# A planner's lag and the first rotation: moving work between VectorE, ScalarE and GpSimd at the start of an attention and mixture-of-experts kernel

## The chip, the cores and the metric

The kernel runs on one core of one Trainium2 chip. The metric is the device time of one execution in microseconds, given as the median of several executions. The profile shows one execution, with times from the start of its span.

## The reference

Four sequences of 1024 tokens with 256 channels go through a layer norm, attention with 16 heads of 16 channels and rotary positions, an output projection, a layer norm and a residual sum. Then follows a layer norm, a mixture of 8 experts of which each token takes the two most distant centroids, a layer norm and a residual sum.

```python
def apply_rope(x):
    ...
    x1, x2 = (x[..., :half], x[..., half:])
    return jnp.concatenate([x1 * cos - x2 * sin, x1 * sin + x2 * cos], axis=-1)
q = (x @ Wq.T + bq).reshape(B, T, H, D)
k = (x @ Wk.T + bk).reshape(B, T, H, D)
v = (x @ Wv.T + bv).reshape(B, T, H, D)
q = apply_rope(q)
k = apply_rope(k)
scores = jnp.einsum('bthd,bshd->bhts', q, k) / np.sqrt(D).astype(x.dtype)
attn = jax.nn.softmax(scores, axis=-1)
out = jnp.einsum('bhts,bshd->bthd', attn, v).reshape(B, T, C)
return out @ Wo.T + bo
```

The expert part is `silu(xs @ Wg[e] + bg[e]) * (xs @ W1[e] + b1[e]) @ W2[e] + b2[e]`, weighted by a softmax of the two chosen distances.

## The kernel before

Attention comes first, for four batches `b`, each with four groups `g` of four heads. A group needs six things in a row. `project` multiplies the normalized, transposed tokens by the query and key weights, and ScalarE copies the result into `turned`. `rotated` adds the bias and applies the rotary positions in five elementwise instructions (`rot`, two `sw`, `rot`, `rot`) for one half of the sequence (512 tokens, `half` 0 or 1) of one group. `split_up` then makes four copies of each of queries and keys: the value cast to a shorter mantissa, the remainder, and both again in an order in which a matmul of the stacked parts gives the full product. That is four instructions for the queries and four for the keys, and the tile is `split`. `stack` transposes the split on TensorE (`ps`), and copies it to `stack`. `maxima` multiplies queries by keys for the row maxima (TensorE `pm`, VectorE `part`, one `peaks()` for two of each), and `rows` turns them into a `shift`. After that, `scores` recomputes the product with the shift (`sc`), ScalarE takes the exponentials (`e`) and TensorE the weighted sums (`av`) with the value tiles `v_aug`. These are 128x512 tiles cleared once by GpSimd, with a column of ones, into which ScalarE copies the values (`pv`).

The beginning is written out by hand. `prepare(..., fast=True)` for both halves of batch 0 runs layer norm statistics on VectorE (`st_a`, then `mv_a`, `var_a`, and the inverse root up to `off_a`), normalization on ScalarE (`xn`), transposes (`pt`), and the projection of group 0 only. `compact` packs weights on ScalarE, `small_constants` makes constants on VectorE, and `turned_constants` prepares `bias_qk` and `turn`. Then `split` and `stack` of group 0 are finished for both halves. Before the change `split` runs half 0 of this first group on GpSimd and half 1 on VectorE, all other groups on GpSimd.

From there on the order of TensorE, VectorE and ScalarE is that of the program text (a manual schedule), and GpSimd's instructions that go through `pool` keep their order too. Other GpSimd instructions, the clearing of the value tiles among them, are placed by the framework's scheduler, which takes the earliest in the program among those that it believes ready. What is in the program text is decided by a planner in Python that keeps one clock for each engine, `free`. Everything beside scores, maxima and weighted sums is a `Work`: a generator that yields, ahead of each part, the costs of the part by engine in ns, as `"G5500"` for 5500 ns of GpSimd or `"P430 A550"` for TensorE followed by ScalarE. `run_one` takes the first of the works, sorted by due time, whose next part fits: its `ready` time must not lie beyond the engine's clock, and the engine may not be booked further ahead of TensorE's clock than `ROOM`. After a part, `ready` is the part's end plus a `LAG` of its engine:

```python
    ROOM = dict(P=10**9, D=1400, A=2600, G=15000)
    LAG = dict(P=280, D=120, A=150, G=200, W=0)
...
            if self.ready > (now if first in "PW" else max(now, free[first])):
                return False
            return all(e == "W" or free[e] + c - now <= ROOM[e] for e, c in costs)
```

So before the change the second part of a work does not fit directly behind its first part on the same engine: `ready` is one lag beyond the clock, until something else moves the clock. A later instruction in another engine's queue waits on the chip for whatever it needs; the planner does not model when a dependent work on another engine has really ended, only that it has been issued.

After attention come the last two blocks' `finish` and `settle` (output projection, layer norms, choice of experts, and the indirect writes of tokens to `rows`), then the expert part over 46 tiles, and the last layer norm.

Of the kernel before, what the change touches and what calls it, by code (L numbers as in the profile page):

```python
# [8 lines left out]
F32 = mybir.dt.float32  # L9
# [7 lines left out]
P = 128  # L17
B, T, C = 4, 1024, 256
NH, HD = 16, 16
NG = 4  # L20
NT = T // P
# [35 lines left out]
def sandwich(  # L57
# [4 lines left out]
    nc = tc.nc  # L62
# [9 lines left out]
    ap1 = attn.enter_context(tc.tile_pool(name="ap1", bufs=1))  # L72
# [54 lines left out]
    def counting(n, name, step=1, per_partition=0):  # L127

        i = ap1.tile([P, n], I32, tag="sq", name=f"i_{name}")
        nc.gpsimd.iota(i, pattern=[[step, n]], base=0, channel_multiplier=per_partition)  # L130
        f = const.tile([P, n], F32, tag=name, name=name)
        nc.gpsimd.tensor_copy(f, i)
        return f
# [6 lines left out]
    zero = ap1.tile([P, 4 * P], F32, tag="oT", name="zero")  # L140
    nc.gpsimd.memset(zero, 0.0)

    v_aug = []
    for t in range(NT):
        v = ap1.tile([P, NH, 32], F32, tag=f"v{t}", name=f"v{t}")
        nc.gpsimd.memset(v, 0.0)
        nc.gpsimd.memset(v[:, :, HD : HD + 1], 1.0)
        v_aug.append(v)  # L150
    tiles_at = counting(P, "tiles_at")
    region = counting(NE, "region", step=CAP)
    part_id = counting(1, "part_id", per_partition=1)
# [151 lines left out]
    seen = const.tile([P, NE], F32, tag="seen", name="seen")  # L305
    nc.gpsimd.memset(seen, 0.0)

    class InOrder:


# [6 lines left out]
    pool = InOrder(nc.gpsimd)  # L317
# [67 lines left out]
    def bank_free(r, n):  # L385
        return max(ring[r][(taken[r] + i) % len(ring[r])] for i in range(n))

    def take(r, until):
        ring[r][taken[r] % len(ring[r])] = until
        taken[r] += 1  # L390

    ROOM = dict(P=10**9, D=1400, A=2600, G=15000)
    LAG = dict(P=280, D=120, A=150, G=200, W=0)
# [3 lines left out]
    class Work:  # L397
# [21 lines left out]
        def run(self):  # L419
            t = self.ready  # L420
            bank_used = self.need[0] == "P"
            if bank_used:
                r = self.costs()[1][0]
                t = max(t, bank_free(r, 1))
            for e, c in self.costs():
                if e != "W":
                    t = max(t, free[e], free["P"] - 300)
                    free[e] = t + c
                t += c + LAG[e]
            if bank_used:  # L430
                take(r, t)
            self.ready = t
            self.need = next(self.gen, None)
            if self.need is None:
                works.remove(self)

        def finish(self):
            for w in self.after:
                w.finish()
            while self.need is not None:  # L440
                self.run()
# [89 lines left out]
    def rotated(b, g, half, e):  # L531

        c = ap2.tile([P, NTB, 8, HD], F32, tag="rot", name=f"rot_{b}_{g}_{half}")
        sw = ap1.tile([P, NTB, 8, 2, HD // 2], F32, tag="B", name=f"sw_{b}_{g}_{half}", bufs=2)
        cols = slice(2 * 4 * HD * g, 2 * 4 * HD * (g + 1))
        at = slice(NTB * half, NTB * half + NTB)
        e.tensor_tensor(
            c.rearrange("p t h d -> p t (h d)"), turned[half][:, :, cols],
            bias_qk[:, None, cols].to_broadcast([P, NTB, 8 * HD]), ALU.add,
        )  # L540
        sh = [P, NTB, 8, HD // 2]
        for s in range(2):
            o = HD // 2 * (1 - s)
            e.tensor_tensor(
                sw[:, :, :, s, :], c[:, :, :, o : o + HD // 2],
                turn[:, at, None, HD + 8 * s : HD + 8 * s + 8].to_broadcast(sh), ALU.mult,
            )
        e.tensor_tensor(
            c, c, turn[:, at, None, :HD].to_broadcast([P, NTB, 8, HD]), ALU.mult
        )  # L550
        flat = c.rearrange("p t h d -> p (t h d)")
        e.tensor_tensor(flat, flat, sw.rearrange("p t h s d -> p (t h s d)"), ALU.add)
        return c

    def split_up(b, g, half, c, e):
        sp_ = ap2.tile([P, NTB, 2, 4, 4, HD], F32R, tag="split", name=f"split_{b}_{g}_{half}")
        for i in range(2):
            full = c[:, :, 4 * i : 4 * i + 4]
            at = lambda n: sp_[:, :, i, :, n, :]
            e.tensor_copy(at(0), full)  # L560
            e.tensor_tensor(at(1), full, at(0), ALU.subtract)
            e.tensor_copy(at(2), at(i))
            e.tensor_copy(at(3), at(1 - i))
        return sp_

    splits = {}

    def split(b, g, half, fast=False):

        e = nc.vector if fast and half else pool  # L570
        yield "G5500"
        c = rotated(b, g, half, e)
        yield "G4000"
        splits[b, g, half] = split_up(b, g, half, c, e)

    def stack(b, g, half, fast=False):

# [595 lines left out]
    def fetch(j):  # L1173
        n = tiles[j]
        e = nc.sync.value_load(tabi[:, 0, j : j + 1], min_val=0, max_val=NE - 1)
        r = nc.sync.value_load(tabi[:, 1, j : j + 1], min_val=0, max_val=NROW - n * P)
        xt = mp.tile([P, NTS, XW], F32, tag="xt", name=f"xt_{j}")
        nc.sync.dma_start(
            out=xt[:, :n], in_=rows[bass.ds(r, n * P), :].rearrange("(i p) c -> p i c", p=P)
        )  # L1180
        w = wpool.tile([P, WW], F32, tag="w", name=f"w_{j}")
        for p, cols in (
            (slice(0, P), slice(0, OR)), (slice(0, FR + 1), slice(OR, WW)),
            (slice(R2, R2 + FR + 1), slice(OR, WW)),
        )[: n + 1]:
            nc.sync.dma_start(
                out=w[p, cols], in_=wall[bass.ds(e, 1), p, cols].rearrange("e p w -> (e p) w")
            )
        return xt, w
# [45 lines left out]
    def down(j, xt, w):  # L1235

        pos = [bank(f"pe_{j}_{i}") for i in range(tiles[j])]
        for i, po in enumerate(pos):
            r = slice(i * R2, i * R2 + FR + 1)
            nc.tensor.matmul(po[:, :C], hr[j % 2][r, :], w[r, OR:], start=True, stop=False)  # L1240
        for i, po in enumerate(pos):
            for f in range(NC):
                nc.tensor.matmul(  # L1243
                    po[:, :C], hs[j % 2][:, f, i * P : (i + 1) * P],
                    w[:, O2 + f * C : O2 + (f + 1) * C], start=False, stop=(f == NC - 1),
                )
            y = mp.tile([P, C], F32, tag=f"y{i}", name=f"yo_{j}_{i}")
            ids = mp.tile([P, 1], I32, tag=f"ids{i}", name=f"ids_{j}_{i}")
            own = sp.tile([P, 1], F32, tag=f"own{i}", name=f"own_{j}_{i}")
            at = xt[:, i, C + 1 : C + 2]  # L1250
            nc.vector.tensor_scalar(
                own, at, float(2 * B * T), float(j * TS), ALU.is_ge, ALU.mult
            )
            nc.vector.tensor_tensor(ids, own, at, ALU.add)
            nc.vector.tensor_scalar(y, po[:, :C], xt[:, i, C : C + 1], None, ALU.mult)  # L1255
            sent = nc.gpsimd.indirect_dma_start(  # L1256
                out=res[:, :],
                out_offset=bass.IndirectOffsetOnAxis(ap=ids, axis=0),
                in_=y,
                in_offset=None,  # L1260
            )
            tc.declare_no_dep(sent.ins, group="results", reason="rows of their own")
            tc.add_to_no_dep_group("results", sent.ins)
            yield
# [12 lines left out]
    with tc.manual_schedule(engines={ET.SP, ET.PE, ET.DVE, ET.Activation}):  # L1277
        ready, last = [fetch(0), fetch(1)], iter(())
        xT = transposed(0, ready[0][0])
        for j in range(MT):  # L1280
# [13 lines left out]
            xT, last = nxt, down(j, xt, w)  # L1294
# [126 lines left out]
```

## Time and profile before

| what | us |
|---|---|
| median of 3 runs | 1761.02 (1759.54 to 1766.38) |
| the profiled execution's own time | 1750.23 |
| its span | 1748.1 |
| first `pm` matmul (row maxima begin) | 42.31 |
| first `sc` matmul (scores begin) | 83.92 |
| last `av` matmuls begin | 1062.61 |
| first expert matmul `pu` on the chain | 1135.30 |

The span is what the engines' instructions cover; the execution's time is 2.1 us longer. In the timelines a line gives the start, the busy time, the engine, the source line, the operation, the output and input by their names, and in brackets the idle time before it and what ended it. `L315` is the line of the helper through which all `pool` instructions pass, so these are told apart by their tiles.

### The profile page before, as it was taken

To read this page: it belongs to the slowest core of one execution; us is meant where nothing else is said; L and a number is where in the kernel's file an instruction comes from. 1 tells how busy PE (TensorE), PEld (TensorE's weight loads), DVE (VectorE), ACT (ScalarE), POOL (GpSimd) and SP (SyncE) were. 2 spreads that over 40 slices of the span, in tenths; PEclk is the share of its full clock that TensorE was granted. 3 is DMA by queue.
4 is the path that set the end of the run, shared out by engine and by line. 5 is a ranking of instruction groups with operands and counts; after the bars stand their busy time and mean duration, and the time that the engine had idled before them with its cause. 6 is when DMAs were issued, how large, how long until landed. Compare 5 with 4: busy or idle time off the path is not lost.

```text
span 1748.1 us, 27778 instructions
## 1 busy us (share of the span) xinstructions
PE 1571.6 (90%) x9702; PEld 1032.8 (59%) x9702; DVE 1062.8 (61%) x2549; ACT 884.2 (51%) x1811; POOL 548.5 (31%) x1058
## 2 busy tenths in 40 slices
PE   3799999999999999999999996199999999999970
PEld 3454455545555545455554443088888888888860
DVE  6487687787787786777787864333333333333338
ACT  2267777778786767676776675021111111122213
POOL 5652434365463454462541223201111111111110
PEclk8899999999999999999999998599999999999995
DMA  8999800001000100000000101544455555578755
GB/s 247 296 301 254 216 28 16 25 25 37 13 14 13 37 21 29 25 1 13 25 29 10 37 13 49 200 172 178 177 186 187 183 186 185 195 280 290 288 191 216
DMA packets 92030, 213.76 MB, mean 122 GB/s; under 512 B 11469, under 2 KB 71092, under 8 KB 86004
## 3 DMA queue, kind: packets, MB, share of 16 engines
q1 hardware_dynamic: 80820, 178.29, 31.1%
q0 software_dynamic: 8768, 25.33, 4.3%
q10 hardware_dynamic: 2304, 8.39, 1.2%
q8 instruction: 76, 1.25, 0.3%
q14 instruction: 62, 0.51, 0.1%
HBM read 148.75 MB, written 80.58 MB: 131 GB/s over the span
## 4 chain that ended last, share of the span: by engine, by line
PE 51%; issue 26%; DVE 12%; POOL 6%; ACT 3%; DMA 2%; SPq 0%; ACTq 0%; POOLq 0%; DVEq 0%
PE av L802 12%; PE pm L644 9%; PE sc L726 7%; DVE part L648 6%; PE sc L733 5%; POOL res L1256 4%; PE pp L510 3%; PE pu L1213 3%; PE ps L585 3%; PE py L833 2%; PE pv L523 1%; PE pd L675 1%; PE pdist L895 1%; PE pe L1243 1%; ACT e L737 1%
## 5 line engine op out<-in xcount | busy, mean ns | idle before, releaser
L648 DVE TENSOR_REDUCE part<-pm 128x1 f32<-128x512 f32 x1024 | 641.4, 682 | 158.4 <-PE pm L644 157.0
L737 ACT ACTIVATE e<-sc 128x512 f32<-128x512 f32 x1024 | 530.5, 603 | 134.4 <-PE sc L733 133.2
L1213 PE MATMUL pu<-xT,w 128*128 128x256 f32 (+3 forms) x2024 | 361.8, 333 | 6.9 <-DMA xt<-rows 4.0
L1213 PEld LDWEIGHTS pu<-xT,w 128*128 128x128 f32 (+1 forms) x2024 | 316.0, 190 | 40.9 <-issue 9.2
L1219 ACT ACTIVATE sil<-pu,w 128x256 f32<-128x256 f32 (+3 forms) x276 | 117.2, 425 | 435.6 <-PE pu L1213 414.1
L644 PE MATMUL pm<-stack,stack 64*128 64x512 f32 x960 | 273.4, 465 | 11.7 <-DVE part L648 8.9
L802 PE MATMUL av<-e,v 128*32 128x512 f32 x2048 | 276.3, 611 | 0.0
L1224 DVE SCALAR_TENSOR_TENSOR h<-pu,w,sil 128x256 f32<-128x256 f32 (+1 forms) x230 | 97.2, 423 | 230.5 <-ACT sil L1219 230.5
L733 PE MATMUL sc<-shift,bring 64*128 64x512 f32 x1024 | 229.0, 402 | 4.1 <-ACT shift L633 4.1
L1256 POOL DMA_INDIRECT res<-yo,ids x71 | 68.1, 959 | 508.6 <-DVE yo L1255 508.6
L726 PE MATMUL sc<-stack,stack 64*128 64x512 f32 x960 | 220.1, 411 | 1.8 <-ACT stack L592 1.0
L644 PEld LDWEIGHTS pm<-stack,stack 64*128 64x128 f32 x960 | 132.6, 185 | 128.3 <-DVE part L648 82.2
L1243 PE MATMUL pe<-w,h 128*128 128x256 f32 x710 | 169.6, 386 | 0.0
L1243 PEld LDWEIGHTS pe<-w,h 128*128 128x128 f32 x710 | 131.0, 190 | 31.2 <-issue 15.2
L726 PEld LDWEIGHTS sc<-stack,stack 64*128 64x128 f32 x960 | 116.2, 187 | 31.8 <-ACT stack L592 8.8
L733 PEld LDWEIGHTS sc<-shift,bring 64*128 64x128 f32 x1024 | 110.2, 187 | 22.8 <-ACT shift L633 7.9
L1255 DVE TENSOR_SCALAR yo<-pe,xt 128x256 f32<-128x256 f32 x71 | 34.3, 483 | 108.4 <-PE pe L1243 108.4
L585 PEld LDWEIGHTS ps<-ident_r,split 128*128 128x128 f32 x512 | 53.1, 145 | 73.4 <-ACT e L737 31.0
L592 ACT CAST stack<-ps 128x512 fp32r<-128x512 f32 x124 | 72.5, 593 | 45.7 <-PE ps L585 43.7
L991 POOL DMA_INDIRECT rows<-xr,to x64 | 63.3, 989 | 71.7 <-DVE to L986 55.7
L585 PE MATMUL ps<-ident_r,split 128*128 128x128 f32 x512 | 69.9, 268 | 16.8 <-POOL split L315 16.8
L802 PEld LDWEIGHTS av<-e,v 128*32 128x32 f32 x2048 | 40.9, 108 | 72.3 <-issue 69.7
(278 smaller groups left out, 1470.5 us busy)
## 6 DMA issues: line engine op xcount, KB each, us to landing
w<-wall SPq DMA_DIRECT2D x46, 2034.0 KB
rows<-empty SPq DMA_DIRECT2D x35, 1032.0 KB
xt<-rows SPq DMA_DIRECT2D x25, 258.0 KB
wall<-in_wg_dram SPq DMA_DIRECT2D x16, 342.0 KB
wall<-in_w_dram SPq DMA_DIRECT2D x16, 320.0 KB
wall<-in_w_dram SPq DMA_DIRECT2D x8, 640.0 KB
xb<-in_x_dram POOLq DMA_DIRECT2D x8, 512.0 KB, 4.3
resid<-xb SPq DMA_DIRECT2D x8, 512.0 KB
```

Source lines behind the costliest of these rows:

```text
L585: nc.tensor.transpose(ps[:, t * P : (t + 1) * P], splits[b, g, half][:, t, is_k, 2 * pr : 2 * pr + 2].rearrange("p h n d -> p (h n d)"), i ...
L644: nc.tensor.matmul(pm, q[r, t * P : (t + 1) * P], k_[r, half * TB : (half + 1) * TB], start=True, stop=True,)
L648: nc.vector.tensor_reduce(part[:, i, 2 * pr + s, half : half + 1], pm, AX.X, ALU.max)
L726: nc.tensor.matmul(sc, k_[r, kb * P : (kb + 1) * P], q[r, qb * TB : (qb + 1) * TB], start=True, stop=False,)
L733: nc.tensor.matmul(scs[s], bring[pr][r, :], shift[u][r, :], start=False, stop=True)
L737: nc.scalar.activation(e, scs[s], AF.Exp, scale=1.0 / HD**0.5)
L802: nc.tensor.matmul(av[32 * j : 32 * j + 32, :], v_aug[kb][:, 4 * g + j, :], es[j], start=(kb == 0), stop=(kb == NT - 1),)
L1213: nc.tensor.matmul(pu[:m, i, :n], w[:, c0 : c0 + m], xT[:, k, :n], start=(k == 0), stop=(k == KC - 1),)
L1219: nc.scalar.activation(sil[:m, :n], pu[:m, 0, :n], AF.Silu, bias=w[:m, OB + f : OB + f + 1])
L1224: nc.vector.scalar_tensor_tensor(h[:, f, :n], pu[:, 1, :n], bias, sil[:, :n], ALU.add, ALU.mult)
L1243: nc.tensor.matmul(po[:, :C], hs[j % 2][:, f, i * P : (i + 1) * P], w[:, O2 + f * C : O2 + (f + 1) * C], start=False, stop=(f == NC - 1),)
L1256: sent = nc.gpsimd.indirect_dma_start(out=res[:, :], out_offset=bass.IndirectOffsetOnAxis(ap=ids, axis=0), in_=y, in_offset=None,)
```

## The change

It does three things. The rotation of the first group goes to VectorE for both halves, and the six casts and copies of each `split_up` there go to ScalarE, with the two subtractions on VectorE; the costs that the planner is told change with it. The clearing of the eight value tiles stands later in the program, behind the other constants that GpSimd makes. And in the planner, a work whose next part begins on the engine on which its last part ended is ready without the lag.

```diff
@@ -140,14 +140,6 @@
     zero = ap1.tile([P, 4 * P], F32, tag="oT", name="zero")
     nc.gpsimd.memset(zero, 0.0)
-    v_aug = []
-    for t in range(NT):
-        v = ap1.tile([P, NH, 32], F32, tag=f"v{t}", name=f"v{t}")
-        nc.gpsimd.memset(v, 0.0)
-        nc.gpsimd.memset(v[:, :, HD : HD + 1], 1.0)
-        v_aug.append(v)
     tiles_at = counting(P, "tiles_at")
@@ -305,6 +297,14 @@
     seen = const.tile([P, NE], F32, tag="seen", name="seen")
     nc.gpsimd.memset(seen, 0.0)
+    v_aug = []
+    for t in range(NT):
+        v = ap1.tile([P, NH, 32], F32, tag=f"v{t}", name=f"v{t}")
+        nc.gpsimd.memset(v, 0.0)
+        nc.gpsimd.memset(v[:, :, HD : HD + 1], 1.0)
+        v_aug.append(v)
     class InOrder:
@@ -427,12 +427,15 @@
                     t = max(t, free[e], free["P"] - 300)
                     free[e] = t + c
                 t += c + LAG[e]
+                last = e
             if bank_used:
                 take(r, t)
-            self.ready = t
             self.need = next(self.gen, None)
             if self.need is None:
                 works.remove(self)
+            elif self.need[0] == last:
+                t -= LAG[last]
+            self.ready = t
@@ -552,26 +555,26 @@
-    def split_up(b, g, half, c, e):
+    def split_up(b, g, half, c, e, copy):
         sp_ = ap2.tile([P, NTB, 2, 4, 4, HD], F32R, tag="split", name=f"split_{b}_{g}_{half}")
         for i in range(2):
             full = c[:, :, 4 * i : 4 * i + 4]
             at = lambda n: sp_[:, :, i, :, n, :]
-            e.tensor_copy(at(0), full)
+            copy(at(0), full)
             e.tensor_tensor(at(1), full, at(0), ALU.subtract)
-            e.tensor_copy(at(2), at(i))
-            e.tensor_copy(at(3), at(1 - i))
+            copy(at(2), at(i))
+            copy(at(3), at(1 - i))
         return sp_
     def split(b, g, half, fast=False):
-        e = nc.vector if fast and half else pool
-        yield "G5500"
+        e, copy = (nc.vector, nc.scalar.copy) if fast else (pool, pool.tensor_copy)
+        yield "D3000" if fast else "G5500"
         c = rotated(b, g, half, e)
-        yield "G4000"
-        splits[b, g, half] = split_up(b, g, half, c, e)
+        yield "D1000 A2200" if fast else "G4000"
+        splits[b, g, half] = split_up(b, g, half, c, e, copy)
```

## The prediction

> **What bounds the kernel now.** I read the windows first, then what TensorE waits for up to the first scores, then the timelines of TensorE, GpSimd and VectorE there. The page's first rows say what an edit away from TensorE can be worth at most:
>
> ```profile
> PE 1571.6 (90%) x9702; PEld 1032.8 (59%) x9702; DVE 1062.8 (61%) x2549; ACT 884.2 (51%) x1811; POOL 548.5 (31%) x1058
> PE   3799999999999999999999996199999999999970
> ```
>
> TensorE is busy in nine tenths or more of nearly every slice. By the windows it is idle for only 26 us of the 976 between 84 and 1060. Time can be had where the first slices are empty. TensorE's waits before the first scores:
>
> ```profile
> PE ps L585 <- POOL split L315: 16.8, 3, 9.1
> PE pt L474 <- ACT xn L356: 16.3, 3, 13.9
> PE pmx L629 <- DVE mx L625: 2.5, 1, 2.5
> ```
>
> The first line is the change's field: TensorE waited 16.8 us in three waits for the split that GpSimd makes. They are 9.1 us at 36.4, 1.5 us at 38.6, and one of 6.2 us later:
>
> ```profile
> 63.15 0.50 PE L644 MATMUL pm<-stack,stack 64*128 64x512 f32 x2
> 69.87 0.75 PE L585 MATMUL ps<-ident_r,split 128*128 128x128 f32 x4 [6.22 <-POOL split L315]
> ```
>
> It belongs to group 1, which stays on GpSimd, where the two halves stand like this:
>
> ```profile
> 57.18 1.26 POOL L315 TENSOR_TENSOR rot<-turned,bias_qk 128x512 f32<-128x512 f32 x1 [18.64 <-ACT turned L515]
> ...
> 62.57 1.27 POOL L315 TENSOR_TENSOR rot<-turned,bias_qk 128x512 f32<-128x512 f32 x1
> ...
> 67.94 0.40 POOL L315 CAST split<-rot 128x256 fp32r<-128x256 f32 x1
> ...
> 71.72 0.40 POOL L315 CAST split<-rot 128x256 fp32r<-128x256 f32 x1
> ```
>
> A new rotation begins at 57.18 and at 62.57, and only then the two splits, at 67.94 and 71.72. Half 0 is rotated at 62.6 and lies there for 5.4 us while half 1 is rotated. The last fence is VectorE, at the head and in the first rotation:
>
> ```profile
> 8.73 1.85 DVE L347 TENSOR_SCALAR var_a<-mv_a 128x4 f32<-128x4 f32 x1
> ...
> 27.33 0.69 DVE L537 TENSOR_TENSOR rot<-turned,bias_qk 128x512 f32<-128x512 f32 x1 [0.79 <-ACT bias_qk L194]
> 28.12 2.15 DVE L544 TENSOR_TENSOR sw<-rot,turn 128x256 f32<-128x256 f32 x2
> 30.31 1.09 DVE L548 TENSOR_TENSOR rot<-rot,turn 128x512 f32<-128x512 f32 x1
> 31.44 1.63 DVE L552 TENSOR_TENSOR rot<-rot,sw 128x512 f32<-128x512 f32 x1
> ```
>
> `var_a` takes 1.85 us where the same form takes 0.17 us at 13.47; GpSimd runs the clearing of the value tiles back to back from 6.17 to 10.63 beside it. The rotation's three full-width instructions take 0.69, 1.09 and 1.63 us for the same number of elements, while GpSimd rotates the other half.
>
> **The planner's lag (part three), where most of the gain is.** With the lag gone, `G4000` of half 0 fits right behind its `G5500`, before half 1's projection is out. GpSimd then runs rotation 0 (57.18 to 62.6), split 0 (3.8 us, to 66.4), rotation 1 (5.4 us, to 71.8), split 1 (to 75.6): the same work in another order. The transposes are ordered by due time behind the same four value projections as now, so TensorE comes to the first of them at 63.65, as before. That transpose needs the queries' half of split 0, done 1.9 us after its start, so at 64.5 and not 69.8: the wait goes from 6.2 to about 0.9 us. What is late next is half 1. Its first transpose (the fifth in all) ran at about 77.9; it now finds its split half done only at 66.4 + 5.4 + 1.9 = 73.7. TensorE would be there at 71 to 72.5 (64.5 plus the 8.0 us that the stretch from 69.87 to 77.9 took, less up to 1.5 us, because two `pv` of 2.04 and 1.63 us there ran after the idle time and later ones take 1.10). So a wait of 1.2 to 2.7 us is left, and the gain is 77.9 - 73.7 = 4.2 us. The sixth transpose needs 75.5 and is reached at 73.7 + 0.4 + 1.0 + 0.45, so in time. From the first scores on TensorE is the bound, and an earlier start carries through. Bounds: nothing, if the planner's room keeps the old order, and 5.4 us, if the fifth transpose is placed later. I take **-4.2**.
>
> **The first rotation (part one).** After: five VectorE instructions without GpSimd beside them, 3 x 0.69 + 2 x 0.43 (a 128x256 `gt` of two inputs takes 0.43) + four gaps of 0.04 = 3.1 us, from 27.33 to 30.4. Then a chain between the two engines for each of queries and keys: ScalarE's cast (0.40 each, from the four `wqk` copies of 128x256 at a mean of 401 ns; 0.31 more for one directly behind), VectorE's subtraction (0.43[...]), the remaining copies. That puts the second subtraction at 32.2 to 32.6. VectorE's queue holds half 1's rotation behind that wait: 32.7 to 35.7. Its casts and subtractions end at 38.0 on VectorE and 38.7 on ScalarE. Now the splits end at 38.5 (GpSimd) and 37.9 (VectorE). So the serial rotation on one engine eats nearly all of what the lost contention gives back. What is gained is order: half 0 is ready at about 33.4, its four transposes (0.43 each) run in the idle time, and only half 1's four are left. They wait for PSUM banks: `stack` copies stand behind the casts in both queues, VectorE's from 38.0 (0.69 each), ScalarE's from 38.7 (0.59), so the first bank in turn comes free at 39.35, and four transposes bring the first `pm` to 41.1, against 42.31. **-1.2**, between +0.5 (copies with strides slower than `wqk`'s) and -2.0.
>
> **The value tiles (part two).** The eight clearings are 8 x 0.51 = 4.1 us of GpSimd. They are moved past the counters' iotas and casts, `empty` (1.82 us, waiting for ScalarE's `wqk` copy until 11.2), the two `natural` DMAs of the GpSimd queue (0.60 and 0.53), `token_id` and `seen`. On SP, the `rows` transfers that need `empty` start at 16.88 behind sixteen `wo` issues that occupy the queue to 16.04, so an earlier `empty` gives nothing there. The tiles are read at 60, so being late costs nothing by itself.
>
> The row says that `var_a` lost 1.68 us to them, at the start of a chain that is tight: the second half's `off_a` at 16.3 holds ScalarE's `xn`, behind which stand all later copies. By the row alone this is -1.7. [...] Today 2.5 us of them, 6.2 to 8.7, lie beside `st_a` statistics, which run at their usual 0.4 us. That cover is gone once they move. Behind 8.7 come `var_a`, `i_a`, `y_a`, `off_a` twice, then 3.4 us of `small_constants`, and blocking a stream of 4.1 us costs up to 4.1 - 1.7 = 2.4 us more than now, 4 at worst if it meets the second `var_a` whole. If it meets only `small_constants`, the copy of `nT` behind it has about 3 us of slack and little is lost. Even `empty` can do it: a `var_a` that is 1.7 us earlier puts the first `off_a` at 11.3, where `empty` now runs from 11.27 to 13.09. So both ends stay: -1.7 and +4. I take **+0.5**, because most placements give back what the row promises.
>
> **The rest of attention.** The lag also changes VectorE's parts: two parts of `settle` or `finish` can now stand in one piece, up to the 1.4 us that `ROOM` allows. That can complete works earlier, and it can put the row maxima behind a burst. Today's waits of `pm` for `part` between 84 and 1090 are 10.0 us in 19, and of `pmx` for `mx` 5.8 us in 4. No row shows the new order; I bound it by -5 and +10 and take 0. At the tail, the final norm's chain on VectorE and ScalarE from 1065 to 1103 is serial and does not change.
>
> **Sum:** -4.2 - 1.2 + 0.5 = -4.9 us. The profiled execution's 1750.2 would become 1745.3. That execution lies 10.8 us under the median of the runs shown, and I carry the difference over to the median: 1761.0 - 4.9 = 1756.1.
>
> **The rivals.** *More is gained:* the value tiles free the head (-1.7), the fifth transpose does not wait (-5.4), rotation -1.5, and some of the 16 us of VectorE waits go (-3): -11.6, about 1749. For it: the waits are there. Against it: every term at its good end. 0.25.
>
> *Little is left:* the clearing meets the second norm chain (+3 to +4) or the split order changes less than I read. About 1760. For it: the `var_a` row shows a full stop. 0.21.
>
> *Slower:* bursts of VectorE parts ahead of the maxima. Each added wait at the mean of today's 19 costs 10.0/19 = 0.53 us of TensorE. Ten of them cancel the gain; it takes 26 to be 0.5% above the median, more than double today's. 30 added give +11, about 1772. For it: VectorE is 72 to 82% busy through attention. Against it: `ROOM` stays at 1.4 us, and the maxima are drawn twelve steps ahead. 0.12.
>
> *Forecast* as worked out, -2.5 to -8.7: 0.42.
>
> **Numbers.** Half a per cent, 8.8 us, is about what a measurement of this kernel can tell from no change; the three runs alone span 6.8 us. Faster by more is the first rival, 0.25; within, the forecast and the second, 0.63; slower, the third, 0.12. The range from 1746 to 1768 takes in the forecast, the second rival and most of the first.
>
> **What would show it.** After: GpSimd's rows of group 1 alternate rotation, split, rotation, split, the wait of `ps` for `split` near 63 is under 2 us, one of 1 to 3 us follows some 8 us later, first `sc` at about 78.5 to 79.5 (83.92 now). First `pm` near 41.6 with the head's 0.5 us in it; GpSimd idle from 27 to 38. `var_a` at 0.17 us, and another VectorE copy or tensor_scalar of over 1 us beside the clearings. Waits of `pm` for `part` near 10 us in the rest of attention. The prediction is wrong if the first scores are not at least 3 us earlier, or if they are and the gain is lost by 1062.

## The result: scores that begin as early as forecast, and a loss in the attention loop

| | before | after |
|---|---|---|
| median of 6 runs each, one chip | 1765.06 us | 1811.47 us (1809.43 to 1818.12) |
| ratio | | 1.0272, 95% interval 1.0248 to 1.0297 |
| span of the profiled execution | 1748.1 us | 1807.4 us |
| first `pm` / first `sc` | 42.31 / 83.92 | 39.40 / 78.56 |
| copy of the first unit's `ou` / of the last of 32 | 119.55 / 1065.21 | 116.79 / 1124.88 |

The forecast was 1756.1, 4.9 us better than before. The kernel came out 2.7% slower, by 46.4 us of the medians. A unit is eight steps of scores for one group and half a sequence, and ends with ScalarE's copy `ou`. By that clock the changed kernel is 2.8 us ahead after the first unit and 59.7 us behind after the last, so the loop lost 62.4 us. That is one execution against one: the profiled execution of before, at 1750.2 us, is a quick one for its kernel, and the difference of the two profiles (59.2 us in time) lies 13 us above that of the medians.

Half of the gain at the start is gone by the end of the first unit: the first `sc` is 5.4 us early, the first `ou` 2.8 us. In between the granted clock of TensorE, as a share of full speed, averages 0.90 (0.95 before), which is 4.0 us of missing clock in place of 1.7.

On the page, the row of busy time and the row of TensorE's slices answer to the two shown first:

```profile
PE 1594.7 (88%) x9702; PEld 1040.0 (58%) x9702; DVE 1072.1 (59%) x2550; ACT 889.1 (49%) x1823; POOL 536.4 (30%) x1045
PE   4899999998989989989998999259999999999970
```

The same 9702 matmuls are busy 23 us longer, and the loop's slices now have eights among the nines. What TensorE waited for up to the first scores, and group 1's transposes there (from TensorE's timeline):

```profile
PE ps L588 <- ACT split L566: 8.4, 3, 4.4
PE ps L588 <- POOL split L315: 4.2, 2, 3.2
...
62.25 0.54 PE L588 MATMUL ps<-ident_r,split 128*128 128x128 f32 x4 [1.00 <-POOL split L315]
...
71.57 0.53 PE L588 MATMUL ps<-ident_r,split 128*128 128x128 f32 x4 [3.15 <-POOL split L315]
```

GpSimd's timeline shows why: the second half's rotation now stands behind the first half's split.

```profile
54.79 1.26 POOL L315 TENSOR_TENSOR rot<-turned,bias_qk 128x512 f32<-128x512 f32 x1 [34.67 <-ACT turned L518]
60.29 0.40 POOL L315 CAST split<-rot 128x256 fp32r<-128x256 f32 x1
...
64.12 1.27 POOL L315 TENSOR_TENSOR rot<-turned,bias_qk 128x512 f32<-128x512 f32 x1
69.64 0.40 POOL L315 CAST split<-rot 128x256 fp32r<-128x256 f32 x1
```

This is the order that the prediction describes: one wait of 6.2 us has become one of 1.0 and one of 3.2, where it had 0.9 and at most 2.7. VectorE at the head:

```profile
8.68 0.17 DVE L347 TENSOR_SCALAR var_a<-mv_a 128x4 f32<-128x4 f32 x1
...
11.25 1.52 DVE L351 TENSOR_SCALAR off_a<-off_a 128x4 f32<-128x4 f32 x1
...
15.71 4.31 DVE L169 TENSOR_SCALAR diag<-ident,bqk 128x64 f32<-128x64 f32 x8
...
26.30 0.69 DVE L540 TENSOR_TENSOR rot<-turned,bias_qk 128x512 f32<-128x512 f32 x1 [0.79 <-ACT bias_qk L186]
...
27.90 0.69 DVE L551 TENSOR_TENSOR rot<-rot,turn 128x512 f32<-128x512 f32 x1
28.62 0.69 DVE L555 TENSOR_TENSOR rot<-rot,sw 128x512 f32<-128x512 f32 x1
```

`var_a` takes 0.17 us in place of 1.85, and the long times have come back at two other groups of tensor_scalars: `off_a` takes 1.52 us (0.17 before) beside `empty` (GpSimd, 10.93 to 12.75), and eight `diag` take 4.31 us (1.40 before) beside the moved clearings (14.3 to 20.1). So `var_a` lost 1.68 us less, and these two lost 1.35 and 2.91 us more. That the clearings would hold up what stands there next was the author's estimate in the prediction; at the head of before one row shows it, `var_a`, which ended at 10.58, beside clearings that ended at 10.63. What the clearings and `empty` did to the path is small: the rotation begins at 26.30 instead of 27.33. Its three full-width instructions take 0.69 us each with GpSimd idle beside them, as forecast (0.69, 1.09 and 1.63 before).

The loss is in the loop. The waits of TensorE and VectorE from 84 us to the end of attention, before (first two lines) and after:

```profile
PE pm L644 <- DVE part L648: 10.0, 19, 1.6
DVE st_m L362 <- POOL xb L315: 2.9, 2, 1.4
```

```profile
PE pm L647 <- DVE part L651: 36.1, 36, 3.3
PE ps L588 <- POOL split L315: 9.9, 2, 5.1
PE sc L729 <- ACT stack L595: 6.8, 3, 4.7
DVE st_m L362 <- POOL xb L315: 16.0, 7, 4.1
DVE st_m L362 <- issue: 4.4, 1, 4.4
```

The columns are the total, the number of waits and the longest. `pm` waits for `part` not many times more often (36 against 19) but for much longer. And a line that was next to nothing is now 16.0 us: VectorE stands still for `xb`. A block is half a sequence (512 tokens), and there are eight. One such place, in the second block, in the joint timeline of after:

```profile
409.08 1.26 POOL L315 TENSOR_TENSOR xb<-xb,outs 128x512 f32<-128x512 f32 x1 [5.26 <-ACT outs L356]
410.37 0.75 DVE L362 BATCH_NORM_STATS2 st_m<-xb 128x6 f32<-128x256 f32 x2 [2.70 <-POOL xb L315]
411.04 2.47 DVE L651 TENSOR_REDUCE part<-pm 128x1 f32<-128x512 f32 x4
...
411.77 0.79 PE L647 MATMUL pm<-stack,stack 64*128 64x512 f32 x1 [2.82 <-DVE part L651]
```

Read from the top: ScalarE is late with the normalized `outs`, for which GpSimd is idle 5.26 us, so its sum `xb` is late; `settle`'s second pair of statistics stands at the head of VectorE's queue and waits 2.70 us for it; the row maxima `part` stand behind it with their inputs ready (the last `pm` ahead of them began at 408.56, `part` at 411.04), and the next `pm` waits 2.82 us for `part`. Before, the last sum of the same block had ended 40 us ahead of its statistics (GpSimd's timeline, then VectorE's):

```profile
369.22 1.27 POOL L315 TENSOR_TENSOR xb<-xb,outs 128x512 f32<-128x512 f32 x1 [0.71 <-ACT outs L356]
...
410.76 0.74 DVE L362 BATCH_NORM_STATS2 st_m<-xb 128x6 f32<-128x256 f32 x2
413.26 0.74 DVE L362 BATCH_NORM_STATS2 st_m<-xb 128x6 f32<-128x256 f32 x2
```

A second price comes with the stall, in the windows around it. The columns are the stretch, its length, each engine's busy time with instructions, and the granted clock of TensorE third from the right:

```profile
408.00:410.80 2.80, 0.95 (x7) 0.50 (x5) 0.43 (x2) 2.80 (x7) 1.26 (x1) 1.00 0.00 0
410.80:417.60 6.80, 5.83 (x16) 2.20 (x17) 3.51 (x12) 1.23 (x3) 2.21 (x12) 0.50 0.24 80
417.60:420.00 2.40, 2.40 (x17) 1.53 (x16) 0.86 (x2) 1.41 (x3) 0.58 (x3) 0.99 0.00 0
```

From 410.8 to 417.6 TensorE has half of its clock (0.50). That is 3.4 us of missing clock, of which 0.5 falls in the wait itself, so by this estimate the wait of 2.82 us costs about as much again. The wait runs from 408.95 to 411.77, and the half clock begins 1.9 us into it.

The windows from the first `ou` to the last, before and then after, account for the loop (the first figure behind the length is TensorE's busy time):

```profile
119.55:1065.21 945.66, 921.52 (x6186) 495.99 (x6186) 723.92 (x1551) 693.25 (x1387) 385.71 (x830) 0.99 0.16 45
```

```profile
116.79:1124.88 1008.09, 943.37 (x6182) 503.15 (x6182) 733.87 (x1555) 693.64 (x1386) 380.83 (x822) 0.96 0.15 42
```

Of the 62.4 us, TensorE is idle for 40.6 (64.7 against 24.1), and busy for 21.9 more with practically the same matmuls. The clock explains the second part: by the trace's clock the busy time misses 31.3 us against 10.2, so 21 more. Of the idle time from 84 to 1060, single waits of 1.7 us or longer make up 39.7 us in 13, against 5.4 us in 3 before; the shorter ones hardly differ (21.6 against 17.3).

The 13 have more than one cause. Nine are waits of `pm` for `part`, 23.3 us in all, of which five stand behind statistics that wait for `xb`. Two are waits of `ps` for a split (9.9 us) and two of `sc` for ScalarE's copy of a stack (6.5 us).

### The profile page after: what moved, and what is told of

It reads as the page before. It is cut to its first block, busy times and chain, and to the rows that moved or that the text cites. A ratio compares the mean times of both kernels' runs of the same rounds, so it can differ in the third digit from the quotient of the medians.

```text
span 1807.4 us, 27782 instructions
## 1 busy us (share of the span) xinstructions
PE 1594.7 (88%) x9702; PEld 1040.0 (58%) x9702; DVE 1072.1 (59%) x2550; ACT 889.1 (49%) x1823; POOL 536.4 (30%) x1045
## 4 chain that ended last, share of the span: by engine, by line
PE 48%; issue 26%; DVE 14%; POOL 6%; ACT 4%; DMA 1%; another core or an unknown queue 0%; SPq 0%; ACTq 0%; POOLq 0%; DVEq 0%
PE av L805 12%; PE pm L647 9%; PE sc L729 6%; DVE part L651 6%; PE sc L736 5%; POOL res L1259 3%; PE pp L513 3%; PE pu L1216 2%; PE ps L588 2%; PE py L836 2%; PE pv L526 1%; ACT e L740 1%; PE pdist L898 1%; PE pd L678 1%; PE pe L1246 1%
## 5 line engine op out<-in xcount | busy, mean ns | idle before, releaser
L647 PE MATMUL pm<-stack,stack 64*128 64x512 f32 x960 | 282.7, 476 | 39.2 <-DVE part L651 34.8
L805 PE MATMUL av<-e,v 128*32 128x512 f32 x2048 | 284.2, 627 | 0.0
```

What stands on the lines that cost most here:

```text
L647: nc.tensor.matmul(pm, q[r, t * P : (t + 1) * P], k_[r, half * TB : (half + 1) * TB], start=True, stop=True,)
L805: nc.tensor.matmul(av[32 * j : 32 * j + 32, :], v_aug[kb][:, 4 * g + j, :], es[j], start=(kb == 0), stop=(kb == NT - 1),)
```

## The experiments

Fourteen kernels ran, in four sets with the kernel before on the same chip. "Loop" below is the change of the last `ou` against the profile of before, less that of the first; one execution against another it is good to about 7 us, since a kernel with the same order on TensorE (the run of the beginning alone) differs by 7.0. The ratios are firmer. The column on `xb` leaves out waits that the trace puts down to "issue".

| run | ratio (95%) | loop us | `st_m` for `xb` us (times) | TensorE waits from 1.7 us up (times) |
|---|---|---|---|---|
| before | 1 | 0 | 2.9 (2) | 5.4 (3) |
| changed kernel | 1.0272 (1.0248 to 1.0297) | +62.4 | 16.0 (7) | 39.7 (13) |
| e1 planner only | 1.0329 (1.0303 to 1.0356) | +64.8 | 16.4 (7) | 38.0 (13) |
| e2 beginning only | 0.9993 (0.9985 to 1.0001) | +7.0 | 2.9 (2) | 9.9 (5) |
| e3 lag off, VectorE | 1.0313 (1.0287 to 1.0339) | +64.9 | 16.0 (7) | 42.8 (10) |
| e4 lag off, GpSimd | 1.0150 (1.0129 to 1.0171) | +35.5 | 2.9 (2) | 24.3 (6) |
| e5 lag off, start | 0.9976 (0.9966 to 0.9986) | -5.6 | 2.9 (2) | 7.5 (4) |
| e6 settle held back | 1.0144 (1.0127 to 1.0161) | +27.5 | none | 23.0 (6) |
| e7 all held back | 1.0033 (1.0017 to 1.0050) | +16.6 | none | 13.2 (3) |
| e14 all but settle held back | 1.0110 (1.0084 to 1.0135) | +29.1 | 12.9 (6) | 16.8 (7) |
| e10 settle joined | 1.0216 (1.0194 to 1.0237) | +31.5 | 8.0 (5) | 30.4 (7) |
| e13 joined, settle held back | 1.0022 (1.0015 to 1.0030) | -4.5 | none | 11.9 (3) |
| e8 ROOM 1300 | 1.0126 (1.0104 to 1.0149) | +23.8 | 5.0 (3) | 17.7 (7) |
| e11 ROOM 1390 | 1.0026 (1.0017 to 1.0036) | +2.5 | 2.9 (2) | 10.7 (3) |
| e12 LAG 1 | 1.0106 (1.0084 to 1.0127) | +22.1 | 8.8 (5) | 16.0 (6) |
| e9 start, and all held back | 0.9953 (0.9938 to 0.9968) | +1.2 | none | 9.3 (2) |

### Which part of the change: e1 to e4

The planner's part alone, on the kernel before; then the other two parts without it (the changed kernel with the old three lines of the planner).

> The kernel before with part three alone (no lag between two parts of a work on one engine). Its TensorE queue is in the order of the changed kernel, entry by entry. All theories: if the loss is part three's alone, 46 us over before plus what the hand-written beginning gives, so +47 to +52 us. If the loss needs the first two parts, within 5 us of before.

> The changed kernel with the old lag: parts one and two alone. TensorE's queue is in the order of before, entry by entry. The changed kernel's first row maxima begin 2.9 us earlier than before (39.4 against 42.3), so -2 to -4 us if an earlier start carries through to the end; 0 if a later wait takes it back.

The planner alone takes 1816.83 us against 1757.55, so it carries the whole loss; TensorE's order in it is that of the changed kernel entry by entry. It loses more than the whole change (59.3 us; 47 to 52 were expected), and why the other two parts are worth that much beside it is not shown. The beginning alone takes 1756.70. Its first `pm` comes at 40.48, 1.8 us early, but without the planner's new order for group 1 the transpose waits 6.25 us for its split as before, and the first `sc` is back at 83.44. So the two parts on their own give next to nothing.

Then the lag was taken away for one engine at a time.

```diff
-            elif self.need[0] == last:
+            elif self.need[0] == last == "D":
```

> The changed kernel with the lag removed only where both parts are on VectorE. Theory A (the lag on GpSimd kept VectorE and TensorE from standing in their queues for GpSimd's results): no loss, -5 to +5 us against before, waits of st_m for GpSimd's xb near 3 us. Theory B (bursts of VectorE parts ahead of the row maxima, the prediction's third rival): most of the loss, +25 to +45. Theory C (any order other than the tuned one is worse): +15 to +45 here and in the GpSimd half alike.

> The changed kernel with the lag removed only where both parts are on GpSimd. Theory A: most of the loss, +30 to +50 us, with waits of st_m for xb and of ps for split as in the changed kernel. Theory B: -8 to +5, the gain of the beginning with little loss. Theory C: +15 to +45, as in the VectorE half.

VectorE's half alone costs as much as everything (1813.61), GpSimd's half about half of it (1784.59). The two do not add up, since each makes a plan of its own, and none of the three theories foretold both. VectorE's half has the stalls for `xb` in full, GpSimd's has none beyond those of before and instead waits of `ps` for the split of up to 8.1 us. That is two kinds of damage: statistics issued ahead of their data, and late splits. The bursts as such, which the prediction's third rival had in mind, exist too: one of the changed kernel's 13 long waits, at 451, stands behind 4.6 us of `settle`'s selection in one piece, planned at 2.0 us (`D400`, twice `D600`, `D400`). One of its instructions, a tensor_scalar whose median over 16 is 0.18 us, takes 1.21 us, with 1.28 us of GpSimd's rotation beside it (447.82 to 449.10):

```profile
447.93 1.21 DVE L938 TENSOR_SCALAR sel<-place 128x32 f32<-128x32 f32 x1
...
451.37 0.50 PE L647 MATMUL pm<-stack,stack 64*128 64x512 f32 x1 [2.67 <-DVE part L651]
```

### The lag taken away at the start alone: e5

```diff
-            elif self.need[0] == last:
+            elif self.need[0] == last and at_step[0] == 0:
```

> The change with the lag taken away only before the attention loop has begun (a condition on the step). The later order differs from that of parts one and two alone in only a few tens of entries of TensorE's queue. If the loss belongs to the new order in the main loop and the 5 us at the start are real and carry: 1750 to 1754, units at -3 to -5 against before all along, first sc at 78.5. If the 5 us are not carried (the main loop is bound by something that starts at a fixed time, or a small perturbation of the order loses as much): 1757 or more, with the difference shrinking to 0 over the first units.

1745.45 against 1750.62 us, a ratio of 0.9976: 5.2 us faster (2.5 to 6.0 by the interval), with the first `sc` at 79.27. TensorE's queue differs from before in the first 19 of 256 steps alone. So the loss belongs to the new order in the loop. That the 5.2 us are the start's gain, carried to the end, is not shown: in the profiles the lead is 4.7 us at the first `sc`, 1.9 at the first `ou` and 2.2 at the 17th, where 3 to 5 were expected all along. The rest of the 7.5 us at the last `ou` was gained later, in an order that is the same as before; from 84 to 1060 this execution misses 5.2 us of clock, that of before 11.9.

### Parts planned before their data exist: e6, e7, e14

The planner's `fits` lets a work begin when the works it follows have no part left to issue. It does not ask when those parts end: `ready` of a new work is its time of creation. The lag covered for that in two ways.

In the first block of a batch (for the first three batches) it kept `settle`'s second pair of statistics back until VectorE's planned clock had moved on, by which time `xb` was there. Without it both pairs go out in the same step, behind a sum that GpSimd has yet to make. The first block, before and then after:

```profile
331.81 0.75 DVE L362 BATCH_NORM_STATS2 st_m<-xb 128x6 f32<-128x256 f32 x2
...
336.07 0.74 DVE L362 BATCH_NORM_STATS2 st_m<-xb 128x6 f32<-128x256 f32 x2
```

```profile
328.11 0.74 DVE L362 BATCH_NORM_STATS2 st_m<-xb 128x6 f32<-128x256 f32 x2
331.15 0.75 DVE L362 BATCH_NORM_STATS2 st_m<-xb 128x6 f32<-128x256 f32 x2 [2.30 <-POOL xb L315]
```

The second block of a batch was covered otherwise, as at 410.76 above. Its `settle` may begin only when the first block's has been issued to the end. By the planner's clocks that was at step 84 of the loop, eleven steps after its own sums; in the changed kernel the first block's ends at step 78, so the second block's goes out in the step of its last sum, 83.

These runs put the missing condition in: for `settle` only (e6), for all works that follow others (e7), and for all of these but `settle` (e14). The filter on the work's name is the only difference.

```diff
         def fits(self):
...
+            if not self.begun:
+                self.ready = max([self.ready] + [w.ready for w in self.after])
```

> The change, with settle's first part not ready before the planned end of the work that it follows. Theory A (settle's first part is put straight behind the block's last sum on GpSimd, for which VectorE then stands still and lets pm wait): the stalls of st_m for xb (16.0 us in 7) go back to about 3, the waits of pm for part from 36 towards 15 to 20, and 15 to 25 of the 46 to 59 us come back: about 1790 to 1800. Theory B (room: parts of settle, done earlier, take the room of the next batch's preparation, so its splits and stacks come late): st_m's stall goes but the time stays over 1800 and the jumps at units 12, 19 and 25 stay. Theory C (any order other than the one in use costs tens of us): anything between 1780 and 1830, without relation to the stalls.

> As the one before, but for every work that follows others (finish, settle and whatever names works to come after). Theory A: at least as good as the one before, 1780 to 1795. Theory B: no better than 1800. Theory C: no relation to the one before, anywhere from 1780 to 1830.

> The changed kernel with the first part held back for every work that follows others except settle (the opposite half of the run that held back settle alone, 1777.8; all together 1758.2). Cause 1: the stalls for xb are there as in the changed kernel (about 16 us in 7) and 25 to 35 us of loss with them, 1780 to 1795. Cause 2: the splits, which follow the preparation, come in time, ps waits under 2 us for split in the loop, and most of the loss is gone, 1760 to 1775.

Held back for `settle` alone, VectorE never waits for `xb` again and the time falls to 1777.83. Of the six long waits left, the longest is one of 8.1 us for a split of batch 2. The changed kernel has it too (5.1 us), where the rotation itself starts late (GpSimd's timeline, then TensorE's):

```profile
497.68 1.29 POOL L315 TENSOR_TENSOR rot<-turned,bias_qk 128x512 f32<-128x512 f32 x1 [16.07 <-ACT turned L518]
...
505.14 0.75 PE L588 MATMUL ps<-ident_r,split 128*128 128x128 f32 x4 [5.06 <-POOL split L315]
```

GpSimd waited 16 us for the projection, so what came late was the preparation of the batch. By the planner's clocks, its norm part (`D900 G3900`), which needs room on VectorE and GpSimd, is issued at step 80 of the loop instead of step 77 for the first half, and at 92 instead of 89 for the second. With the parts of the previous block able to follow each other at once, the block is finished sooner and the next batch, which is urgent, later. That the one brings the other about is read from the plan; no run tests it by itself. Held back for all works but `settle`, the waits for the split are gone and the stalls for `xb` are there (12.9 us), at 1770.76; held back for all, both are gone, at 1758.17. So each of the two kinds of damage can be taken away by itself, and taking away both brings back 42 of the 48 us by the ratios (2.72% and 0.33% of 1758). e6 and e7 came out faster than their first theory had it (1790 to 1800 and 1780 to 1795); e14 has the stalls of its first cause at the time of its second. Each of the three also makes a new order, and what that alone costs or gives is not taken out. Held back for all, 0.33% of loss remains in spite of a first `sc` at 75.54: its loop is 16.6 us worse than before, three long waits of 13.2 us among it. The longest is one of 7.4 us for the next batch's normalized tokens (`pt` for `xn`); why it comes is not shown.

### The stall alone, put in and taken out: e10, e13

The clearest pair is on the kernel before, with its lag, and one edit. Then the same with `settle` held back as above.

```diff
-        yield "D660"
+        yield "D1320"
         statistics(stats, xb, (0, 1))
-        yield "D660"
         statistics(stats, xb, (2, 3))
```

> The kernel before, lag in force, but settle's two statistics parts are one part (D1320 for twice D660), as they stand in the changed kernel. Theory A: VectorE stands still for xb in about seven blocks again, 14 to 18 us by the waits, TensorE's pm behind it, its clock lower after each, and it costs 20 to 35 us: 1771 to 1786. Theory B: the stall is there but the time moves by under 8 us, because the loss lies in the lateness of the next batch. Theory C: slower by about the 20 us that the other ROOM cost, with no more wait for xb than there.

> The run with settle's two statistics parts joined (1788.9, +37.8), with settle's joined part held back to the planned end of the block's finish. Cause 1 (VectorE's standing still for xb, 8.0 us in 5, and what it makes of pm and the clock): the stalls vanish and at least half of the 37.8 us come back, 1755 to 1770. Cause 2 (the next batch's split comes late, TensorE's ps waits 9.8 us for it at the first unit of batch 2, which joining brought about through the room it takes): the wait of ps for split stays at 8 to 10 us and the time over 1775.

Joining the two parts changes no cost that the planner is told, and it costs 37.8 us on the chip (1788.94 against 1751.13). With the joined part held back to the planned end of the works it follows (its block's sums and the earlier `settle`s), 33 of them come back (1755.97). TensorE's waits in the first and in the second:

```profile
PE pm L644 <- DVE part L648: 20.7, 26, 3.3
PE ps L585 <- POOL split L315: 12.0, 2, 9.8
```

```profile
PE pm L650 <- DVE part L654: 12.6, 21, 2.2
PE ps L591 <- POOL split L315: 6.9, 1, 6.9
```

The piece of 1.3 us by itself costs little (4.8 us is left); when it stands ahead of its data it is dear. Fewer statistics waited than expected (8.0 us in 5 and not 14 to 18 in about 7), and the five are all in first blocks of a batch: in the second blocks the lag still covers, as told above. The wait of 9.8 us for a split of batch 2 went with the stall, and one of 6.9 us came up elsewhere, so late splits are not wholly independent of it. So 33 us is the price of the stall with what it draws along, the change of order included. In the changed kernel, taking the stall away is worth 22 us (e6: 2.72% - 1.44% = 1.28%), and where the splits are no longer late, 14 us (e14 against e7: 0.77%).

### What any other order costs: e8, e11, e12

```diff
-    ROOM = dict(P=10**9, D=1400, A=2600, G=15000)
-    LAG = dict(P=280, D=120, A=150, G=200, W=0)
+    ROOM = dict(P=10**9, D=1300, A=2600, G=15000)   # e8; e11: D=1390
+    LAG = dict(P=280, D=1, A=1, G=1, W=0)           # e12 alone, with D=1400
```

> The kernel before with ROOM for VectorE 1300 in place of 1400 and nothing else: a new order (about as many places of TensorE's queue differ from before as with the change), with the lag untouched. Theories A and B: within 8 us of before, 1750 to 1766, because neither early parts nor their crowding are in it. Theory C: slower by 15 to 45 us, as each of the lag's orders was.

> The kernel before with ROOM for VectorE 1390 in place of 1400: a nearly meaningless edit that still alters some 270 lines of a comparison of TensorE's queue. Theory C: slower by 10 to 30 us. Otherwise within 5 us of before. It measures what being a different order costs by itself.

> The kernel before with LAG 1 in place of 120, 150 and 200 for VectorE, ScalarE and GpSimd, the rule for the next part as before. If it is the planned time of 0.12 and 0.2 us that matters: about as slow as the planner's part alone, 1790 to 1820. If what matters is that a part on the same engine can be taken in the very step of the one before, which 1 ns also nearly allows: likewise slow, with the stalls for xb (over 10 us). If only exact zero does it, st_m waits for xb under 5 us and the time is that of any other order: 1755 to 1775.

`ROOM` of VectorE at 1390 instead of 1400 costs 4.6 us, at 1300 it costs 22 us, although the lag is in force and VectorE waits for `xb` only 5.0 us. So the order in use is better than these two neighbours, and part of what a change of the plan costs is simply that. The third theory held to that extent: a `ROOM` of 1300 costs nearly half of the change's loss by the ratios (1.26 of 2.72%), and the runs do not divide it further. With `LAG` at 1 ns, 18.6 us are lost and about half of the stalls are there (8.8 us in 5), which lies between the outcomes written down for it: the next part still has to wait until something has moved the clock, and that by itself protects only in part.

### A version that beats both: e9

The lag taken away at the start only, and every work's first part held back to the planned end of the works it follows.

> The run with the lag off at the start only (1745.5 against 1750.6), and in it every work's first part is held back to the planned end of the works it follows, with the lag in force. Theory A (parts planned before their data exist make VectorE stand still): the lag's order has only two such stalls left, 2.9 us in all, so little can be gained: 1742 to 1748. Theory C (any other order costs): 1760 to 1790, as about as many places of TensorE's queue change as with the change itself.

1742.45 against 1751.13 us, ratio 0.9953 (0.9938 to 0.9968). The order differs from before in more places than the changed kernel's does, and it is faster. The waits of `pm` for `part` in the loop stay where they were:

```profile
PE pm L653 <- DVE part L657: 11.5, 23, 0.9
```

So a new order need not cost anything. That nothing stands ahead of its data is not enough for that, as e7 shows with the same condition. The first `sc` comes at 74.50, 9.4 us early (20 of the transposes ahead of it now stand behind it), and the last `ou` 9.3 us early. In between the lead was lost, with 0.5 us behind at the 17th `ou`, and won back, so it is not simply the start's gain carried along.

## Why the prediction was wrong, by its steps

**The sum for the beginning held, its terms did not.** First `sc` came 5.4 us early where 4.9 was forecast. The rotation, from its start to the first `pm`, gained 1.9 us (14.98 to 13.10; forecast 1.2, end of the range 2.0). The head gained 1.0 where the value tiles were put at +0.5: the long times did move on to later tensor_scalars, as the upper end of +4 us assumed, but 4.3 us of them fell on `diag`, ahead of a copy of `nT` with slack, and only 1.5 us on the chain. The planner's order gained 2.5 us where 4.2 was forecast, for the fifth transpose waited 3.15 us and not 1.2 to 2.7. Two gains put too low and one too high cancelled, which was luck. And "an earlier start carries through" did not hold in full: 2.8 of the 5.4 us were left at the first `ou`. e5's 5.2 us are near the forecast of 4.9, but only some 2 of them can be followed from the start.

**"The rest of attention", bound by -5 and +10 and taken as 0, is the step that failed.** It measured +62 in the profiles (the medians moved by +46 in all). The third rival had the place and the direction, VectorE's work ahead of the maxima, and was given a chance of 0.12. Three things were wrong.

First, the price of a wait. The third rival took 10.0/19 = 0.53 us for each added wait and asked for 26 of them. There were 17 more of `pm` for `part`, and all of them together took 26 us more. The right unit was the long wait: nine of 1.7 us and up, at a mean of 2.6 us, and four more for splits and stacks at 4.1 us, which the rival did not count at all. In the kernel before, no wait of `pm` for `part` is longer than 1.6 us, so their mean says nothing of such waits.

Second, the mechanism. It looked for bursts of planned work ahead of the maxima and held against them that "`ROOM` stays at 1.4 us". `ROOM` limits what VectorE is planned to do and not how long it stands still. A piece of 1.3 us of statistics that waits 2.7 us for GpSimd holds the maxima up for 4 us (406.93 to 411.04 in the changed kernel), and the planner books 1.3. The text on the kernel said that the planner does not model when a dependent work has ended, and this was never set against the lag: the lag was, unsaid, what covered for it. The row that should have asked the question is the 2.9 us of `st_m` for `xb`, which was in the trace of before. GpSimd's own order does it too. In the fourth block, `xb` was finished late because the indirect writes of the block before it stood ahead of it:

```profile
677.54 0.96 POOL L994 DMA_INDIRECT rows<-xr,to  x1 [0.30 <-issue]
678.51 1.28 POOL L315 TENSOR_TENSOR xb<-xb,outs 128x512 f32<-128x512 f32 x1
...
679.82 0.75 DVE L362 BATCH_NORM_STATS2 st_m<-xb 128x6 f32<-128x256 f32 x2 [4.45 <-issue]
681.22 0.79 PE L647 MATMUL pm<-stack,stack 64*128 64x512 f32 x1 [2.71 <-DVE part L651]
```

The trace puts this wait down to "issue", but the statistics start 0.03 us after GpSimd's sum ends. By the planner's clocks, all four parts of those writes (`G2600` each) are issued in one step (142); before, they were spread over three (146 to 148).

Third, the clock. Twelve of the 13 long waits come with a stretch of 3.4 or 6.8 us at half the clock. By the trace's clock the loop's busy time misses 21 us more than before (31.3 against 10.2), a third of the loop's loss, and the prediction has no term for it.

**What told it apart.** The prediction said that it would be wrong if the first scores came early and the gain was lost by 1062, and that the waits of `pm` for `part` would stay near 10 us. The first `sc` came at 78.56, within the range named for it, the last `ou` 59.7 us late, and the waits were 36.1 us in 36.

## What to carry to other kernels

A delay in a hand-made plan that seems only to waste time may stand for a dependency that the plan does not know: before taking it away, list what follows each delayed part on its engine's queue and ask when its input really ends on the other engine. VectorE ran its queue in the planned order here, and one such part, 2.70 us late at 410.37, made everything behind it wait, with 2.82 us of `pm` at the end; so price it by the longest chain that can stand there and not by the mean wait of the tuned kernel. A change that is right in one stage is best confined to that stage (e5), or made together with the condition that the delay stood for (e9).

## What the runs showed of the hardware that was not expected

Of the 13 single waits of TensorE of 1.8 to 5.1 us in the changed kernel's loop, twelve are followed, or met while they last, by a granted clock of one half for 3.4 or 6.8 us, as from 410.8 to 417.6 above. From 84 to 1060 there are 13 such stretches after the change (the one at 96.8 behind a wait of 1.16 us) and six before. In the kernel before, a wait of 1.86 us that ends at 639.58 is followed by a clock of 0.51 from 641.3 to 648.2. In these traces the length of one wait does not decide it alone. After a wait of 1.92 us that ends at 333.44 in the changed kernel, the clock stays at 1.00; in the kernel before, two waits of 1.21 and 0.38 us between 706.0 and 709.6 are followed by 0.51 up to 713.0. In a loop in which TensorE was 97% busy (921.5 of 945.7 us before), the clock that goes missing with the waits, here 21 us beside 40.6 of idle time, is not in any list of waits.
